# Scan phase of a two-layer image kernel: VectorE's half of the gate placed between two products, a z ring of six loaded two chunks ahead, a softplus ring of two

## The chip, the cores and the metric

The kernel runs on one core of one Trainium2 chip. The metric is device time in microseconds (us), the median of three runs. One further execution was taken by the hardware profiler; its page and trace are the source of every other number here. Five engines work side by side on a core: PE (TensorE, the matrix unit; its weight loads are shown as PEld), DVE (VectorE), ACT (ScalarE), POOL (GpSimd) and SP (SyncE, which here only issues DMAs). They wait for each other by semaphores, and each carries out its own instructions in the order in which they stand.

## The reference, cut to what matters

Input x is 8 images of 128 x 128 positions with 128 channels. Layer 0 is a linear attention block with a layer norm; layer 1 is a 2D selective scan (256 inner channels, one state per channel), and it is layer 1's last part that the change concerns:

```
xz = x @ Win;  xb, z = split(xz)                      # 256 channels each
xb = silu(depthwise_conv3x3(xb) + conv_b)
xs = [xb, reversed xb, turned xb, reversed turned xb] # 4 directions, L = 16384 positions
delta = softplus(dt_weight @ (Wxproj_dt @ xs) + dt_bias);  dA = exp(delta * A)
h[t] = dA[t] * h[t-1] + delta[t] * u[t] * B[t];   y[t] = h[t] * C[t] + u[t] * D
y = y0 + y1 + y2 + y3                                 # directions summed, each put back in place
yz = y * silu(z)                                      # the gate
out = layernorm(yz) @ Wout
```

The norm is over the 256 channels, so its mean and variance are sums over partitions, which PE takes with a matrix of 1/256.

## The kernel before, in words

Three stages follow each other. `layer0` computes layer 0 and silu(z), which goes to memory as `zs`. `layer1_front` does the convolution, the sums with D (`gs`), the products with B (`ubs`) and the small rows of the projection (`xps`). `layer1_scan` (from line 688) does the rest; only it is changed.

`layer1_scan` works in units. A unit is one chunk of 1024 positions (CH) of one scan: 8 output images x 4 directions ("places" 0 to 3) x 16 chunks (NCH) make 512 units. The sum y of one image, 256 channels x 16384 positions, stays in SBUF (`y`). Place 0 writes y, places 1 to 3 add to it. While place 0 of the next image runs over y, chunk by chunk, the finished image leaves just ahead of it: each of the 16 leaving steps takes one chunk of 1024 positions, as two pieces of 512 (hf 0 and 1), through gate, norm, projection and store.

The order of the work is written out by hand in `step(n)`; the block under `in_order` keeps every engine's instructions exactly in the order in which the program issues them. A step of unit n does the following. The line numbers are those of the profile.

- `emit(n - 1, hf)` on DVE: the products of the scan's result with C, which PE has spread over the partitions in PSUM (`pc`). In place 0 both halves go straight to y (L915, DVE). In the others half 0 goes to PSUM (L927 or L931) and `gather` adds it to y (L939); half 1 is made in `ubt` (L920), and POOL adds it (`add`, L946).
- `load_rows(n + 2)` (L851, L852) and `load` (ubt of unit n + 3, L858) on SP's queue. In place 0 ("first") `load` stands near the top of the step, in the others at its end.
- `decay` on ACT (exp, L877), `weigh` on POOL (ubt times softplus, L880), both halves of the channels.
- `scan(n, 0)` and `scan(n, 1)` on DVE (L887, L889).
- `delta(n + 1)` on PE (L869), `soften(n + 1)` on ACT (softplus, L873). Softplus and exp need different tables, so each step has two table loads on ACT.
- `spread` on PE (L903), C for the products of the next step.

For the image that leaves, with `now` the chunk of this step, `last` that of the step before and `soon` that of the next:

- `fetch` (L962, SP): both z pieces of a chunk, 512 KB each. The table `fetched` says in which step. Ring of five pieces.
- `gate` (L966): z := y * z, a piece of 2 x 512 on 128 partitions. Half 0 on POOL, half 1 on DVE, both at the end of the step before the chunk's own.
- `square` (L969, ACT) of both halves, written over y; `moments` (L979, PE); `keep` (L985, ACT) copies them; `to_tokens` (L991, PE); `square_mean` (L995, ACT, called mv); `variance` (L999, DVE), the last DVE work of a step but for the gate; `deviation` (L1003 and L1004, a power, POOL).
- `project` (L1011, PE): 32 small matmuls into a PSUM buffer of the ring of three (`px`).
- `store` in the next step (L1017, DVE, eight instructions in two buffers r; L1021, SP).
- `add_d` (L842, a DMA that POOL issues): adds the D sums `gs` to y in memory order, a chunk of 1 MB at a time, from 13 steps before the image leaves to 10 steps into the leaving.

`project` and `delta` share the ring `px`; `moments`, `to_tokens` and half 1 of `spread` share one PSUM bank (tag `pt`). After the last unit 17 more steps only let the last image leave.

The table of fetches before, with n the first leaving step of an image and j the chunk:

```
fetched[n + j - 2 if j > 1 else n + j - 4] = e
```

Of the kernel before, what the change touches and what calls it, by code (L numbers as in the profile page):

```python
# [8 lines left out]
F32 = mybir.dt.float32  # L9
# [7 lines left out]
P = 128  # L17
# [4 lines left out]
NC2 = 2  # L22
R = 8
K = 4
GW = 4
GN = GW * H
# [3 lines left out]
CH = 1024  # L30
CW = CH // H
NCH = L // CH
# [7 lines left out]
def split3(nc, parts, x):  # L40

    for j in range(3):
        nc.vector.tensor_copy(parts[j], x)
        if j < 2:
            nc.vector.tensor_tensor(x, x, parts[j], ALU.subtract)
# [640 lines left out]
def layer1_scan(ctx: ExitStack, tc, ubs, xps, zs, gs, dtw, dtb, a_log, gamma, beta, w_out, out):  # L686
# [15 lines left out]
    nc = tc.nc  # L702
    const = ctx.enter_context(tc.tile_pool(name="l2c", bufs=1))
    big = ctx.enter_context(tc.tile_pool(name="l2b", bufs=1))
    wp = ctx.enter_context(tc.tile_pool(name="l2w", bufs=3))
# [14 lines left out]
    D2 = 2 * P  # L720
    wparts = dram.tile([3, R, K, D2], BF16, name="wparts")
    bparts = dram.tile([3, K, D2], BF16, name="bparts")
    for dst, src, rows in ((wparts, dtw.rearrange("k r d -> r k d"), R), (bparts, dtb.rearrange("o (k d) -> o k d", d=D2), 1)):
        x = wp.tile([rows, K, D2], F32, name="w32", tag="sp", bufs=3)
        nc.sync.dma_start(x, src)
        q = wp.tile([rows, 3, K, D2], BF16, name="w16", tag="ub", bufs=4)
        split3(nc, [q[:, j] for j in range(3)], x)
        for j in range(3):
            if rows == 1:
                nc.sync.dma_start(dst[j : j + 1], q[:, j])  # L730
            else:
                nc.sync.dma_start(dst[j], q[:, j])
# [8 lines left out]
    for i in range(3):  # L741
        t = const.tile([P, CH], BF16, name=f"rows{i}")
# [3 lines left out]
    for i in range(2):  # L746
        t = const.tile([P, D2], BF16, name=f"dtw{i}")
# [23 lines left out]
            nc.vector.memset(sel[at : at + 1, hf, j : j + 1], 1.0)  # L771
    pb = pe.tile([P, P], F32, name="pbw", tag="pt")
    for c in range(NC2):
        bt = wp.tile([P, P], F32, name="bt", tag="z", bufs=5)
        nc.vector.tensor_copy(bt, gb[:, 1, c : c + 1].to_broadcast([P, P]))
        nc.tensor.matmul(pb, bt, wg[:, c, :], start=(c == 0), stop=(c == NC2 - 1))
    bw = const.tile([P, P], F32, name="bw")
# [59 lines left out]
    ubt, sp, da, st = {}, {}, {}, {}  # L837
# [6 lines left out]
    def load_rows(n):  # L844
        sl, i = units[n]
        m = sl.at(i)
        rw = rws[n % 3]
        md = NCH - 1 - m if sl.dt_turned_back else m
        src = xps[sl.dt_image, sl.dt_order].rearrange("j r l -> (j r) l")
        for j in range(3):  # L850
            nc.sync.dma_start(rw[3 * NR * j : 3 * NR * j + 3 * NR, :], src[:, md * CH : md * CH + CH])  # L851
        nc.sync.dma_start(rw[96:99, :], xps[sl.b, sl.order, :, R + 1, m * CH : m * CH + CH])  # L852

    def load(n):
        sl, i = units[n]
        m = sl.at(i)
        ubt[n] = wp.tile([P, NC2, CH], F32, name="ubt", tag="ub", bufs=4)
        nc.sync.dma_start(ubt[n], ubs[sl.b, sl.order].rearrange("c p l -> p c l")[:, :, m * CH : m * CH + CH])  # L858
# [10 lines left out]
            nc.tensor.matmul(p[:, hf * 512 : hf * 512 + 512], sl.dw[:, c * P : c * P + P], src, start=True, stop=True)  # L869

    def soften(n, c):
        sp[n, c] = t = wp.tile([P, CH], F32, name="sp", tag="sp", bufs=3)
        nc.scalar.activation(t, da[n, c], AF.Softplus)  # L873

    def decay(n, c):
        sl, i = units[n]
        nc.scalar.activation(da[n, c], sp[n, c], AF.Exp, scale=sa[:, sl.s, c : c + 1])  # L877

    def weigh(n, c):
        nc.gpsimd.tensor_tensor(ubt[n][:, c, :], ubt[n][:, c, :], sp.pop((n, c)), ALU.mult)  # L880
# [24 lines left out]
    def emit(n, hf):  # L905

        sl, i = units[n]
        h = ubt[n][:, :, hf * 512 : hf * 512 + 512]  # L910
        c = cps.pop((n, hf)).to_broadcast([P, NC2, GN])
        if sl.place == 0:
            v = sl.y_at(i, hf)
            split = "p c (a b) -> p c a b"
            nc.vector.tensor_tensor(v, h.rearrange(split, b=H), c.rearrange(split, b=H), ALU.mult)  # L915
            if hf == 1:
                ubt.pop(n)
            return
        if hf == 1:
            nc.vector.tensor_tensor(h, h, c, ALU.mult)  # L920
            return
        p = da.pop((n, 1))
        if sl.y_turned:
            ts[n] = p.rearrange("p (c b a) -> p c b a", c=NC2, a=GW)
            t = p.rearrange("p (c b a) -> p c a b", c=NC2, a=GW)
            split = "p c (a b) -> p c a b"
            nc.vector.tensor_tensor(t, h.rearrange(split, b=H), c.rearrange(split, b=H), ALU.mult)  # L927
        else:
            t = p.rearrange("p (c q) -> p c q", c=NC2)
            ts[n] = t.rearrange("p c (a b) -> p c a b", b=H)  # L930
            nc.vector.tensor_tensor(t, h, c, ALU.mult)  # L931

    def gather(n):

        sl, i = units[n]
        v = sl.y_at(i, 0)
        if sl.y_turned:
            v = v.rearrange("p c a b -> p c b a")
        nc.vector.tensor_tensor(v, v, ts.pop(n), ALU.add)  # L939
# [9 lines left out]
    zt, rst, pts, mv = {}, {}, {}, {}  # L949

    def piece(m, hf):
        return y[:, :, (2 * m + hf) * GN : (2 * m + hf + 1) * GN]

    def mirrored(o, m, hf):
        p = 2 * m + hf
        return 2 * NCH - 1 - p if o % 2 == 1 else p

    def fetch(o, m):
        for hf in range(2):
            zt[m, hf] = z = wp.tile([P, NC2, GN], F32, name="z", bufs=5)  # L960
            p = mirrored(o, m, hf)
            nc.sync.dma_start(z, zs[o].rearrange("c p l -> p c l")[:, :, p * GN : p * GN + GN])  # L962

    def gate(o, m, hf, eng):
        z, ym = zt[m, hf], piece(m, hf)
        eng.tensor_tensor(z, ym[:, :, ::-1] if o % 2 == 1 else ym, z, ALU.mult)  # L966

    def square(m, hf):
        nc.scalar.activation(piece(m, hf), zt[m, hf], AF.Square)  # L969
# [31 lines left out]
    def deviation(m):  # L1001
        rstd = rst[m]
        nc.gpsimd.tensor_scalar(rstd, rstd, 0.0, EPS1, ALU.max, ALU.add)  # L1003
        nc.gpsimd.tensor_tensor(rstd, rstd, half, ALU.pow)  # L1004
# [20 lines left out]
    leaving, summed, fetched = {}, {}, {}  # L1025
    for o in range(B):
        n = (o + 1) * K * NCH
        for j in range(NCH):
            e = o, NCH - 1 - j if o % 2 == 1 else j
            leaving[n + j] = e  # L1030
            fetched[n + j - 2 if j > 1 else n + j - 4] = e
            summed[n - NCH + 3 + (3 * j + 1) // 2] = e
    N = len(units)

    def step(n):
        live = 0 <= n < N
        then = n + 1 < N
        before = 1 <= n <= N
        now, last, soon = (leaving.get(n + i) for i in (0, -1, 1))
        first = before and units[n - 1][0].place == 0  # L1040
        if before:
            emit(n - 1, 0)
            if not first:
                gather(n - 1)
            emit(n - 1, 1)
        if n + 2 < N:
            load_rows(n + 2)
        if first and n + 3 < N:
            load(n + 3)
        if live:  # L1050
            for c in range(NC2):
                decay(n, c)
            weigh(n, 0)
        if last:
            deviation(last[1])
        if live:
            weigh(n, 1)
        if now:
            for hf in range(2):
                square(now[1], hf)  # L1060
            moments(now[1])
        if live:
            scan(n, 0)
            da.pop((n, 0))
        if last:
            for hf in range(2):
                store(*last, hf)
        if then:
            for c in range(NC2):
                delta(n + 1, c)  # L1070
        if now:
            keep(now[1])
        if then:
            for c in range(NC2):
                soften(n + 1, c)
        if now:
            to_tokens(now[1])
            square_mean(now[1])
        if live:
            scan(n, 1)  # L1080
            state(n)
        if now:
            variance(now[1])
        if live:
            spread(n, 0, "pc")
            spread(n, 1, "pt")
        if soon:
            gate(*soon, 0, nc.gpsimd)
            gate(*soon, 1, nc.vector)
        if now:  # L1090
            p = da.pop((n, 1)) if live else px.tile([P, CH], F32, name="px")
            for hf in range(2):
                project(now[1], hf, p[:, hf * 512 : hf * 512 + 512])
        elif live and units[n][0].place == 0:
            da.pop((n, 1))
        if before and not first:
            add(n - 1)
        if n + 3 < N and not first:
            load(n + 3)
        if live and units[n][1] == 1 and n - 1 + NCH < N:  # L1100
            units[n - 1 + NCH][0].weights()
        if n in summed:
            add_d(*summed[n])
        if n in fetched:
            fetch(*fetched[n])

    with in_order(tc):
        units[0][0].weights()
# [74 lines left out]
```

## Time and profile before

| what | value |
|---|---|
| median of 3 runs (lowest, highest) | 9721.64 us (9711.85, 9731.27) |
| profiled execution, its own time | 9691.45 us |
| its span, first to last instruction | 9689.7 us |
| DVE busy | 8237.5 us, 85% of the span |
| POOL busy | 7180.5 us, 74% |
| ACT busy | 7126.3 us, 74% |
| PE busy | 6369.1 us, 66% |
| DMA | 1851.21 MB, mean 191 GB/s |
| L966 on DVE: 128 instructions, mean (shortest, longest) | 2.263 us (1.221, 4.630) |
| L966 on POOL: 128 instructions, mean | 2.375 us |
| POOL's L966 waited for z | 100.6 us in 36 waits |
| DVE's L966 waited for z | 28.9 us in 21 waits |
| L999 on DVE waited for ACT's mv | 79.1 us in 49 waits |
| L1017 on DVE waited for the store of r | 25.4 us in 9 waits |

How to read it. Busy time is the time in which an engine has an instruction under way; an instruction that has started and then stands for a shared resource counts as busy. A line of the timeline gives start and duration in us, engine, line of the code, operation, out<-in, shapes and count, and in brackets how long the engine was idle before it and what ended that. The letter q after an engine's name means its sequencer: SPq L962 is the issue of z's load. A stretch's line has its two ends, its length, and then the busy times named with it. A waits line has who waited for whom: the sum in us, how often, and the longest.

### The profile page before, as it was taken

How to read it: one execution, taken by the hardware profiler on the slowest of the kernel's cores; microseconds unless marked ns; L12 is line 12 of the kernel's file. 1: busy time of each engine (PE TensorE's matmuls, PEld its weight loads, DVE VectorE, ACT ScalarE, POOL GpSimd, SP SyncE). 2: the span in 40 equal slices, each digit the busy share in tenths (PEclk: the TensorE clock that was granted, in tenths of full speed). 3: DMA queues.
4: the chain of work that ended last, by engine and by line, in shares of the span. 5: the costliest groups of instructions: out<-in, count | busy, mean ns of one | idle time of the engine just before them, and what ended most of it. 6: DMA issues, size and time to landing. Idle time of an engine off the chain costs nothing. (4 is left out here: it accounts for less than half of the span.)

```text
span 9689.7 us, 89952 instructions
## 1 busy us (share of the span) xinstructions
PE 6369.1 (66%) x24352; PEld 3134.8 (32%) x24352; DVE 8237.5 (85%) x8676; ACT 7126.3 (74%) x8226; POOL 7180.5 (74%) x4352
## 2 busy tenths in 40 slices
PE   8999999998877779777633634536355363543636
PEld 5555555554332223222200402304022040321403
DVE  6557775565988889888899999999999999999996
ACT  5556565555887778877788787787878878787784
POOL 3445554445575569776679899898989989899897
PEclk9999999999998889888855856658566585665857
DMA  2332233323576679887755948668486684957858
GB/s 90 133 131 86 86 133 131 132 99 117 195 253 225 235 267 247 262 262 266 271 161 170 267 149 232 202 177 255 152 239 194 189 246 152 257 179 193 238 155 214
DMA packets 1034807, 1851.21 MB, mean 191 GB/s; under 512 B 274852, under 2 KB 500772, under 8 KB 1026112
## 3 DMA queue, kind: packets, MB, share of 16 engines
q1 hardware_dynamic: 999488, 1711.23, 54.2%
q0 software_dynamic: 34816, 134.23, 7.1%
q8 instruction: 199, 3.26, 0.1%
q14 instruction: 304, 2.49, 0.1%
HBM read 1153.03 MB, written 692.12 MB: 190 GB/s over the span
## 5 line engine op out<-in xcount | busy, mean ns | idle before, releaser
L880 POOL TENSOR_TENSOR ubt<-ubt,sp 128x1024 f32<-128x1024 f32 x1024 | 2446.6, 2437 | 188.8 <-ACT sp L873 163.1
L869 PE MATMUL px<-rows,dtw 128*128 128x512 bf16 x2048 | 947.9, 564 | 2251.3 <-DVE y L939 1014.6
L504 POOL TENSOR_TENSOR tap<-tap 128x1024 f32<-128x1024 f32 x512 | 1206.8, 2368 | 634.3 <-ACT tap L502 516.7
L512 DVE SCALAR_TENSOR_TENSOR acc<-xb,cw,acc 128x1024 f32<-128x1024 f32 x1024 | 1320.4, 1289 | 52.7 <-DVE acc L512 0.5
L873 ACT ACTIVATE sp<-px 128x1024 f32<-128x1024 f32 x1024 | 1035.2, 1024 | 408.0 <-PE px L869 325.9
L946 POOL TENSOR_TENSOR y<-y,ubt 128x512 f32<-128x512 f32 x768 | 1156.2, 1542 | 149.8 <-DVE ubt L920 148.2
L494 PE MATMUL acc<-xi,wt 128*128 128x512 f32 x2048 | 952.7, 608 | 383.5 <-ACT ures L519 383.1
L869 PEld LDWEIGHTS <-dtw 128*128 128x128 bf16 x2048 | 166.8, 110 | 3070.2 <-issue 960.7
L887 DVE TENSOR_TENSOR_SCAN ubt<-px,state,ubt 128x1024 f32<-128x1024 f32 x480 | 1105.5, 2334 | 4.9 <-issue 3.6
L889 DVE TENSOR_TENSOR_SCAN ubt<-px,state,ubt 128x1024 f32<-128x1024 f32 x480 | 1104.3, 2334 | 6.1 <-issue 3.6
L877 ACT ACTIVATE px<-sp,sa 128x1024 f32<-128x1024 f32 x1024 | 1103.3, 1109 | 6.1
L502 ACT ACTIVATE tap<-xb,cw 128x1024 f32<-128x1024 f32 x768 | 834.3, 1139 | 68.6 <-POOL tap L504 67.5
L873 ACT ACT_TABLE_LOAD x512 | 656.9, 1283 | 226.0 <-PE px L869 207.9
L274 POOL TENSOR_TENSOR q<-q,qs 128x512 f32<-128x512 f32 x256 | 271.1, 1059 | 669.0 <-DVE qs L273 667.8
L494 PEld LDWEIGHTS acc<-xi,wt 128*128 128x128 f32 x2048 | 384.0, 192 | 928.4 <-ACT ures L519 485.6
L877 ACT ACT_TABLE_LOAD x512 | 656.9, 1283 | 9.4
L1011 PEld LDWEIGHTS px<-wg,z 128*128 128x128 f32 x4096 | 588.8, 229 | 165.5 <-issue 159.5
L903 PE MATMUL pc<-rows,csel 128*128 128x512 bf16 x1024 | 516.4, 585 | 129.3 <-DVE rstd L999 126.6
L1011 PE MATMUL px<-wg,z 128*128 128x128 f32 x4096 | 587.4, 312 | 0.0
L467 PE MATMUL pxb<-xi,wi 128*128 128x512 f32 x1024 | 496.2, 607 | 4.5 <-ACT xb L476 4.3
L939 DVE TENSOR_TENSOR y<-y,px 128x1024 f32<-128x1024 f32 x384 | 468.6, 1220 | 14.2
L290 ACT ACTIVATE sq<-o 128x512 f32<-128x512 f32 x256 | 161.2, 630 | 421.6 <-DVE o L288 420.4
(158 smaller groups left out, 15323.6 us busy)
## 6 DMA issues: line engine op xcount, KB each, us to landing
ubt<-ubs SPq DMA_DIRECT2D x512, 1024.0 KB
zs<-z SPq DMA_DIRECT2D x512, 256.0 KB
ubs<-ures SPq DMA_DIRECT2D x256, 512.0 KB
ubs<-turned SPq DMA_DIRECT2D x256, 512.0 KB
y<-gs POOLq DMA_DIRECT2D x128, 1024.0 KB, 11.9
z<-zs SPq DMA_DIRECT2D x256, 512.0 KB
rows<-xps SPq DMA_DIRECT2D x1536, 60.0 KB
xi<-x SPq DMA_DIRECT2D x120, 576.0 KB
```

The lines of the kernel that those rows point to most:

```text
L494: nc.tensor.matmul(acc[:, s, :], wt[:, j, c, :], x, start=(j == 0), stop=(j == len(ON_PE) - 1))
L502: nc.scalar.activation(t, at(n, c, *d), AF.Copy, scale=cw[:, c, tap(*d) : tap(*d) + 1])
L504: nc.gpsimd.tensor_tensor(sums[n, c], sums[n, c], t, ALU.add)
L512: nc.vector.scalar_tensor_tensor(acc, at(n, c, *d), cw[:, c, tap(*d) : tap(*d) + 1], acc, ALU.mult, ALU.add)
L869: nc.tensor.matmul(p[:, hf * 512 : hf * 512 + 512], sl.dw[:, c * P : c * P + P], src, start=True, stop=True)
L873: nc.scalar.activation(t, da[n, c], AF.Softplus)
L877: nc.scalar.activation(da[n, c], sp[n, c], AF.Exp, scale=sa[:, sl.s, c : c + 1])
L880: nc.gpsimd.tensor_tensor(ubt[n][:, c, :], ubt[n][:, c, :], sp.pop((n, c)), ALU.mult)
L887: nc.vector.tensor_tensor_scan(e[:, ::-1], x[:, ::-1], e[:, ::-1], start, ALU.mult, ALU.add)
L889: nc.vector.tensor_tensor_scan(e, x, e, start, ALU.mult, ALU.add)
L946: nc.gpsimd.tensor_tensor(v[:, c], v[:, c], h[:, c], ALU.add)
L1011: nc.tensor.matmul(po[:, w, :], z[:, c, w * H : w * H + H], wg[:, c, :], start=(c == 0), stop=(c == NC2 - 1))
```

## The change

Four edits, all in `layer1_scan`:

1. DVE's half gate of a chunk moves from the end of the step before (`gate(*soon, 1)`, after the scans and the variance) into the chunk's own step, after `emit(n - 1, 0)` (and `gather`, where there is one) and ahead of `emit(n - 1, 1)`. POOL's half stays where it was. The DVE instructions are the same in number and kind.
2. The fetch of z moves from the end of a step to a place behind `load_rows` and `load`, so ahead of the store of r in SP's queue. Chunks 3 to 15 are still fetched two steps ahead of their own; chunks 0, 1 and 2 are fetched 20 steps before their own step, which is in the last four steps of place 2. Before, chunks 0 and 1 were fetched four steps ahead, and chunk 2 two.
3. The z ring has six pieces (three chunks) instead of five.
4. The softplus ring has two buffers instead of three; 4 KB per partition go from one ring to the other.

```diff
-        sp[n, c] = t = wp.tile([P, CH], F32, name="sp", tag="sp", bufs=3)
+        sp[n, c] = t = wp.tile([P, CH], F32, name="sp", tag="sp", bufs=2)
...
-            zt[m, hf] = z = wp.tile([P, NC2, GN], F32, name="z", bufs=5)
+            zt[m, hf] = z = wp.tile([P, NC2, GN], F32, name="z", bufs=6)
...
-            fetched[n + j - 2 if j > 1 else n + j - 4] = e
+            fetched[n + j - (2 if j > 2 else NCH + 4)] = e
...
             emit(n - 1, 0)
             if not first:
                 gather(n - 1)
+        if now:
+            gate(*now, 1, nc.vector)
+        if before:
             emit(n - 1, 1)
         if n + 2 < N:
             load_rows(n + 2)
         if first and n + 3 < N:
             load(n + 3)
+        if n in fetched:
+            fetch(*fetched[n])
...
         if soon:
             gate(*soon, 0, nc.gpsimd)
-            gate(*soon, 1, nc.vector)
...
         if n in summed:
             add_d(*summed[n])
-        if n in fetched:
-            fetch(*fetched[n])
```

The two other edited lines give the setup's tiles of the same rings (w32 and bt) the new ring sizes.

More of the change, by code (lines that the diff above doesn't have):

```diff
@@ L723, in layer1_scan @@
     for dst, src, rows in ((wparts, dtw.rearrange("k r d -> r k d"), R), (bparts, dtb.rearrange("o (k d) -> o k d", d=D2), 1)):
-        x = wp.tile([rows, K, D2], F32, name="w32", tag="sp", bufs=3)
+        x = wp.tile([rows, K, D2], F32, name="w32", tag="sp", bufs=2)
         nc.sync.dma_start(x, src)
@@ L773, in layer1_scan @@
     for c in range(NC2):
-        bt = wp.tile([P, P], F32, name="bt", tag="z", bufs=5)
+        bt = wp.tile([P, P], F32, name="bt", tag="z", bufs=6)
         nc.vector.tensor_copy(bt, gb[:, 1, c : c + 1].to_broadcast([P, P]))
```

## The prediction

> **What bounds the kernel now.** I read the busy table and the 40 slices first, then stretches, then the timeline of single steps, then the waits. The scan phase runs from 4870 us to 9538 us: 512 steps, and a tail of 17. The stretches are one image position of 64 steps: place 0 (16 steps in which the finished image also leaves), places 1, 2, 3, the next place 0, and the tail. Columns: length, busy time of PE, weight loads, VectorE, ScalarE, GpSimd, PE clock, DMA share, GB/s.
>
> ```profile
> 5382.90:5574.40 191.50, 146.99 (x969) 106.28 (x966) 180.61 (x230) 148.28 (x161) 162.97 (x88) 0.90 0.91 269
> 5574.40:5708.90 134.50, 49.49 (x123) 12.11 (x121) 132.36 (x104) 109.31 (x97) 125.35 (x64) 0.53 0.49 152
> 5708.90:5840.30 131.40, 46.78 (x97) 9.00 (x96) 130.17 (x97) 108.33 (x96) 125.33 (x64) 0.50 0.49 152
> 5840.30:5976.70 136.40, 46.07 (x97) 9.45 (x98) 131.72 (x98) 107.05 (x96) 125.98 (x74) 0.50 0.82 218
> ...
> 9538.20:9689.70 151.50, 122.15 (x896) 85.59 (x896) 63.32 (x163) 43.90 (x64) 90.04 (x59) 0.93 0.78 205
> ```
>
> Places 1 and 2 are packed: 8.2 us a step, VectorE 99% busy. What the change touches lies in place 0 (12.0 us a step), the end of place 3, and the tail. But VectorE's 94% in place 0 is not all work. A clean gate, with what GpSimd does beside it, and a bad one:
>
> ```profile
> 5559.72 2.35 POOL L880 TENSOR_TENSOR ubt<-ubt,sp 128x1024 f32<-128x1024 f32 x1 [1.38 <-ACT sp L873]
> ...
> 5560.84 2.31 DVE L966 TENSOR_TENSOR z<-y,z 128x1024 f32<-128x1024 f32 x1
> ...
> 5562.03 1.23 POOL L1003 TENSOR_SCALAR rstd<-rstd 128x8 f32<-128x8 f32 x1
> ```
>
> ```profile
> 6676.73 2.36 POOL L966 TENSOR_TENSOR z<-y,z 128x1024 f32<-128x1024 f32 x1 [2.08 <-DMA z<-zs]
> ...
> 6679.02 1.27 POOL L842 DMA_DIRECT2D y<-gs  x1
> ...
> 6679.41 2.78 SPq L962 DMA_DIRECT2D z<-zs  x2
> 6679.46 4.33 DVE L966 TENSOR_TENSOR z<-y,z 128x1024 f32<-128x1024 f32 x1
> ...
> 6679.89 2.81 POOL L880 TENSOR_TENSOR ubt<-ubt,sp 128x1024 f32<-128x1024 f32 x1
> ...
> 6682.23 1.67 POOL L1003 TENSOR_SCALAR rstd<-rstd 128x8 f32<-128x8 f32 x1
> ```
>
> The gate's own work is 1.1 to 1.2 us (shortest of all 128: 1.221). In the clean case it stands 1.2 us until GpSimd's product (L880) ends at 5562.07, then runs while L1003, which lasts 0.24 us alone at 6659.14, is stretched to 1.23. In the bad case z landed late, GpSimd's half gate and its DMA issue slid, and L880 took the port first: 4.33 us. At the end of place 3 (PE, then VectorE), and the two other waits that matter:
>
> ```profile
> 6553.14 1.87 PE L869 MATMUL px<-rows,dtw 128*128 128x512 bf16 x4 [7.97 <-DMA rows<-xps]
> ...
> 6555.47 1.23 DVE L931 TENSOR_TENSOR px<-ubt,pc 128x1024 f32<-128x1024 f32 x1 [1.60 <-PE pc L903]
> ```
>
> ```profile
> 6651.58 1.12 DVE L1017 SCALAR_TENSOR_TENSOR r<-px,rstd,bw 128x128 f32<-128x128 f32 x4 [1.77 <-DMA out<-r]
> ```
>
> ```profile
> SPq L962 <- PE px L1011: 54.0, 13, 6.2
> ```
>
> The last is SP's own wait in one place 0 (6571 to 6765): 54 us at the head of the z loads, with rows, ubt and everything else behind.
>
> **What the Trainium skill says.** "SBUF — State Buffer", Who interferes with whom: a VectorE instruction with two SBUF inputs contends with a GpSimd instruction that reads SBUF, and the second fully blocks. The two gates above agree (2.31 and 4.33 against 1.22); the products with pc in PSUM show no such spread (1.21 us). "DMA: Bandwidth & Descriptors", Queues, rings and completion order: each DMA engine consumes a ring in order; so a small load issued behind z waits for it. The 7.97 us above, with z issued 5.6 us before, fits. "Perfetto Trace Analysis", GPSIMD Engine Instruction: take GpSimd times from start to start; two L880 in a row give 2.35 us that way (4.70 for the pair), as their spans say.
>
> **The change, part by part.** *The loop that stays.* I measure from the end of the variance (L999), V, to the next. In a clean step ScalarE runs: table load and decays to V+3.25, squares to V+5.2, waits for the moments until V+7.15, copy, table load, softplus, mean square at V+11.1, then V'. None of this moves. PE adds a second leg: projection to V+4.0 at full clock, V+5.6 or V+6.8 at a lower one, then 1.9 us of moments. So a step can't go below about max(7.15, projection end + 1.92) + 4.2. Over the 105 intervals of seven place 0s the timeline gives 11.99 us on average, this formula, fed with each one's projection end, 11.66; 27 intervals lie over 0.3 us above it.
>
> *Gate between the products.* VectorE's work without the gate is 9.0 us start to start (products 2.27, scans 4.56, r 2.05, small ones 0.15). The gate now starts at V+1.17. When ScalarE sets the pace, L880 ends at V+1.25 (softplus half 0 ends 1.2 us before V, plus 2.44), so I take 0.1 us of lock wait and 1.1 us of work: VectorE needs 10.2 us instead of 11.25, and is no longer the limit. The gate ends at V+2.4, before square half 1 is due at V+4.25: nothing is late behind it. The second product, queued behind it, ends at V+3.5 instead of V+4.65, so the bank of the moments and the ubt slot come free sooner. Bounds: no wait, 10.1 us; a gate that meets the power (L1004, 1.66 us) instead waits up to 1.7, VectorE then needs 11.8.
>
> *Loads two chunks ahead.* SP's order was rows, ubt, out, z, z waiting for this step's projection; now rows, ubt, z, out, the slot freed a step before. z is issued near V+5 of step n for GpSimd's gate near V'+6.6, 13 us instead of about 5. The late-z gates go: 35.2 us over 105 intervals, all that the formula leaves. The DMA engines are at 0.91 over place 0 and above 1.0 for steps at a time, so I take **28 us**; bounds 0 and 83 (every step at 11.2).
>
> *z of three chunks loaded before place 3.* It leaves the last four steps of place 3, where gs and z together made rows late, and goes into place 2 (share 0.49, about 4.0 us of 8.2 a step; another 1 MB at about 270 GB/s is 3.9, for three steps: it fits, cost 0; bound 1 us a step). From the scan of the last but one step to V of the leaving step took 17.1 us (6549.1 to 6566.2); two clean steps less the products are 12.9, and GpSimd's gate (2.35) and DMA issue (1.2), which stay, leave it about 0.6 late: 13.5. 8 × 3.6 = **28 us** (bounds 10 and 36).
>
> *First leaving step.* V to V was 14.3 us (6566.20 to 6580.48), since softplus was late after the rows; with rows in time squares end near V+5.8 (two products, gate, square), so 12.2. 7 × 2.1 = **15 us** (bounds a loss of 5, since GpSimd is in L880 then and the gate may stand 2.4 us; a gain of 20).
>
> *Tail.* 16 steps in 151.5 us. PE alone needs 7.35 (9612.07 to 9619.42); GpSimd's gate stood up to 9.8 us for its z (9604.46), issued at the end of the step before. With z ahead PE needs 16 × 7.35 = 118, the DMA engines 0.78 × 151.5 = 118. Both can't be packed: 131, **20 us** (bounds 0 and 30).
>
> *Softplus ring of two.* Softplus half 1 now waits for GpSimd's product of the step before: in place 2 that ends at 5708.74, the softplus starts at 5712.39. 3.6 us of cover: 0. If GpSimd fell 4 us behind, ScalarE would wait the rest, and decays, squares and the scan behind it (bound 1 us at 8 boundaries).
>
> Sum: 28 + 28 + 15 + 20 = 91 us, so the profiled execution (9691.45, span 9689.7 and 1.8 around) would be 9600. It lies 30 us under the median; from 9721.64 the same 91 give **9631**.
>
> **Rivals.** (1) *PE and DMA follow at once*: every drain step near 11.3, boundaries and tail at their bounds, 73 + 36 + 20 + 30 = 159: 9563. For it: ScalarE's loop. Against: DMA share, the projections at lower clock. (2) *The transfers are the limit*: place 0 stays near 12.0 because DMA is already full, and only boundaries and half the tail gain: 28 + 10 = 38: 9684. For it: shares of 1.0 and more over several steps; against: steps of 11.2 at a share of 1.02. (3) *Slower: out lands behind z.* r has two buffers, so a step can't be shorter than the landing time of an out plus 1.2 us. out now stands behind 1 MB of ubt and 1 MB of z. If an out takes over 10.8 us, the step passes 12.0; at 13 us it is 14.2, in the 11 steps with gs: 2.2 × 11 × 7 = 169, less 28 + 15 + 20: 106 us slower, 9828. For it: the 1.77 us above, and loads of 10 to 15 us in the chain. Against: ubt, z and gs were as many before, and only 25 us went to this wait in all.
>
> **Chances.** Forecast 0.62 (9590 to 9675), rival 1 0.13, rival 2 0.16, rival 3 0.09. About 0.2% (19 us) is what a measurement tells from no change. Of rival 2's 0.16, 0.09 lies beyond that and 0.07 within; of rival 3's 0.09, 0.01 within: faster 0.84, same 0.08, slower 0.08. The range reaches to rival 1 and past rival 2: 9568 to 9708.
>
> **What would show it.** Right: gates of VectorE near 1.2 to 1.4 us; no wait of either gate for z; SP's wait for the projection gone; L999 waiting for mv about 0.8 us in each step; rows no longer late at the ends of place 3, place 3 near 132 us; place 0 near 186; tail near 131. Wrong: gates still at 2.3 (the meeting with L880 or L1004); r waiting for out step after step; softplus waiting for GpSimd in places 1 and 2.

## The result, and the profile after

| what | before | after |
|---|---|---|
| median of 15 runs (lowest, highest) | 9709.78 us (9698.72, 9731.27) | 9696.08 us (9684.92, 9708.34) |
| ratio, 95% interval | | 0.9984 [0.9977, 0.9991] |
| span of the profiled execution | 9689.7 us | 9696.4 us |
| first scan to the end | 4819.8 us | 4814.7 us |
| tail, end of the last scan to the end | 151.5 us | 143.8 us |
| VectorE waited for z / GpSimd waited for z | 28.9 / 100.6 us | 0 / 1.9 us |
| L999 waited for mv | 79.1 us | 139.3 us |
| r (L1017) waited for the store of r | 25.4 us | 93.8 us |

The kernel became faster by 14 us; 91 were forecast. (The forecast of 9631 us was counted from a median of 3 runs; that of 15 lies 12 us lower.) The span of the profiled run says nothing on this: 12 us of it lie ahead of the first scan, in code that the change doesn't touch, and the profiled execution of before was 18 us faster than its median, that of after 2 us slower. So I compare from the first scan on, and trust the medians for the total. The same stretches as before, with the same columns: places 0 to 3 and the tail.

```profile
5396.40:5586.30 189.90, 150.11 (x963) 108.48 (x980) 163.11 (x232) 145.30 (x159) 159.21 (x86) 0.86 0.84 258
5586.30:5719.60 133.30, 47.40 (x111) 10.55 (x112) 132.13 (x103) 109.14 (x97) 125.31 (x64) 0.52 0.49 152
5719.60:5851.00 131.40, 46.13 (x95) 9.02 (x96) 130.16 (x96) 108.34 (x96) 125.33 (x64) 0.50 0.56 176
5851.00:5989.50 138.50, 45.07 (x93) 8.94 (x94) 137.26 (x97) 110.13 (x98) 129.62 (x75) 0.50 0.83 212
...
9552.50:9696.40 143.90, 115.37 (x896) 81.50 (x896) 60.23 (x164) 43.35 (x63) 91.73 (x58) 0.95 0.81 212
```

VectorE lost 17.5 us of busy time in place 0 (180.6 to 163.1), but place 0 lost 1.6 us only. Place 3 is longer, 138.5 in place of 136.4, and its added time is booked as VectorE work (137.3 in place of 131.7). Place 2 takes the early z (share 0.56 in place of 0.49) at no cost.

First what went as forecast, in the timeline of one step: the gate starts 0.2 us before the product L880 ends (6592.22 + 2.35 = 6594.57) and lasts 1.28 us. 120 of VectorE's 128 gates are now 1.21 to 1.30 us long.

```profile
6592.22 2.35 POOL L880 TENSOR_TENSOR ubt<-ubt,sp 128x1024 f32<-128x1024 f32 x1 [4.56 <-ACT sp L873]
...
6594.38 1.28 DVE L966 TENSOR_TENSOR z<-y,z 128x1024 f32<-128x1024 f32 x1
...
6594.55 1.22 POOL L1003 TENSOR_SCALAR rstd<-rstd 128x8 f32<-128x8 f32 x1
```

Now the first gate of the same image, one step earlier in the same timeline:

```profile
6575.05 5.53 POOL L880 TENSOR_TENSOR ubt<-ubt,sp 128x1024 f32<-128x1024 f32 x2
...
6576.85 7.11 DVE L966 TENSOR_TENSOR z<-y,z 128x1024 f32<-128x1024 f32 x1
...
6579.66 3.21 POOL L966 TENSOR_TENSOR z<-y,z 128x1024 f32<-128x1024 f32 x1
6583.88 1.21 DVE L920 TENSOR_TENSOR ubt<-ubt,pc 128x1024 f32<-128x1024 f32 x1
6584.00 1.06 ACT L969 ACTIVATE y<-z 128x1024 f32<-128x1024 f32 x1 [5.22 <-DVE z L966]
```

It needs 1.1 us of work and takes 7.11. It ends at 6583.96, which is 1.09 us after GpSimd's own half gate ends (6582.87): it stood through two products and that gate, and ScalarE waited 5.22 us for it. It is so in seven images (7.11 to 7.22 us); the eighth took 2.61. Before the change this gate took 1.40 to 1.43 us in all eight; the same one in the timeline of before:

```profile
6563.56 3.47 POOL L946 TENSOR_TENSOR y<-y,ubt 128x512 f32<-128x512 f32 x2
...
6564.49 1.41 DVE L966 TENSOR_TENSOR z<-y,z 128x1024 f32<-128x1024 f32 x1
```

The second surprise is the store. The timeline of the third leaving step, of SP's queue and VectorE:

```profile
6611.90 0.39 SPq L858 DMA_DIRECT2D ubt<-ubs  x1
...
6612.62 0.89 SPq L962 DMA_DIRECT2D z<-zs  x2
...
6613.48 1.22 POOL L842 DMA_DIRECT2D y<-gs  x1
6613.60 1.57 SPq L1021 DMA_DIRECT2D out<-r  x2
...
6627.05 2.16 DVE L1017 SCALAR_TENSOR_TENSOR r<-px,rstd,bw 128x128 f32<-128x128 f32 x8 [5.38 <-DMA out<-r]
```

The store is issued at 6613.60 behind 1 MB of ubt and 1 MB of z, and the next r can be written only at 6627.05, 13.4 us later. In the packet records of the trace, the store's 1024 packets of 512 B (512 KB, both halves) move between 6623.9 and 6627.0, after ubt (6612.9 to 6617.8) and beside the last of z (6616.5 to 6625.5). Most of that time went by beside the 1 MB of gs: from 6619 to 6623 its packets took 0.80 to 0.82 of the 16 engines' time and those of z 0.23 to 0.25, and the store stood behind z. What the wait would be without gs no run tells, since none moves gs. The variance-to-variance interval of this step is 16.1 us on the mean of seven images, 13.3 before. The waits of the whole run:

```profile
DVE rstd L999 <- ACT mv L995: 139.3, 113, 5.7
...
DVE r L1017 <- DMA out<-r: 93.8, 33, 9.8
...
POOL z L966 <- DMA z<-zs: 1.9, 2, 1.5
```

Where the time went, in us, from the starts of the scans. "Start" is the eleven steps from ten before an image leaves to its first leaving step, of seven images; "leaving" the other 15 steps of place 0, of seven images; "end" the last ten steps with the tail. "Forecast" sorts the prediction's terms the same way (28 × 7/8 + 15; 28; 20 + 28/8; the ring 0).

| | before | after | difference | forecast |
|---|---|---|---|---|
| start | 716.6 | 706.5 | -10.1 | -39.5 |
| leaving | 1243.7 | 1257.7 | +14.0 | -28 |
| end | 232.7 | 222.3 | -10.4 | -23.5 |
| all other steps | 2626.7 | 2628.1 | +1.4 | 0 |

One profiled run scatters in these sums: b2 below, which measures like the kernel before, has 719.7, 1255.5, 232.0, 2630.4. Against b2, "leaving" of the changed kernel is only 2.2 us longer. So the +14 is weak by itself; that the -28 is missing is not.

### The profile page after: what moved, and what is told of

It is laid out like the page before. It is cut to its first block, busy times and chain, and to the rows that moved or that the text cites. A ratio compares the mean times of both kernels' runs of the same rounds, so it can differ in the third digit from the quotient of the medians.

```text
span 9696.4 us, 89952 instructions
## 1 busy us (share of the span) xinstructions
PE 6347.2 (65%) x24190; PEld 3133.0 (32%) x24352; DVE 8158.9 (84%) x8676; ACT 7127.9 (74%) x8226; POOL 7169.8 (74%) x4352
## 5 line engine op out<-in xcount | busy, mean ns | idle before, releaser
L880 POOL TENSOR_TENSOR ubt<-ubt,sp 128x1024 f32<-128x1024 f32 x1024 | 2433.4, 2429 | 266.7 <-ACT sp L873 248.4
L869 PE MATMUL px<-rows,dtw 128*128 128x512 bf16 x1893 | 912.6, 575 | 2191.0 <-DVE y L939 1029.3
L873 ACT ACTIVATE sp<-px 128x1024 f32<-128x1024 f32 x1024 | 1037.0, 1024 | 441.2 <-PE px L869 354.1
L946 POOL TENSOR_TENSOR y<-y,ubt 128x512 f32<-128x512 f32 x768 | 1147.2, 1529 | 169.3 <-DVE ubt L920 164.6
L939 DVE TENSOR_TENSOR y<-y,px 128x1024 f32<-128x1024 f32 x384 | 468.6, 1220 | 14.2
```

The lines of the kernel that those rows point to most:

```text
L946: nc.gpsimd.tensor_tensor(v[:, c], v[:, c], h[:, c], ALU.add)
```

## The experiments

Three theories. **P, the port:** the first gate of an image is caught behind GpSimd's unbroken train of work, and pays for most of what the earlier rows bring. **Q, the queue:** the store of r, now issued behind z, lands too late for the next r. **R, the transfers:** the DMA engines are full in place 0, in whatever order things are issued. All ratios are to the kernel before on the same chip.

**a1, first gate back at the end of the step before** (only chunk 0's):

```diff
-        if now:
+        if now and last:
             gate(*now, 1, nc.vector)
...
             gate(*soon, 0, nc.gpsimd)
+            if not now:
+                gate(*soon, 1, nc.vector)
```

> The changed kernel with one thing put back: chunk 0's half gate on VectorE stands at the end of the step before, as in the kernel before; chunks 1 to 15 stay between the products. Theory P (the shared port): in the changed kernel that first gate stands about 5.9 us behind GpSimd's three products and gates in a row, in 7 images; put back, it takes about 1.4 us, the step from the scan before it to the next goes from 15.3 back to near 9.6 us, and the time falls by 30 to 40 us against the changed kernel, to a ratio of about 0.995 with the kernel before. Theory Q (out behind z): the first gate is cheap to remove but the step after it is held by other waits; at most 10 us fall. Theory R (the transfers are full anyway): what the gate gives back is lost again in the next steps to waits for out; 0 to 10 us.

9694.14 us, ratio 0.9982 [0.9975, 0.9989]: nothing gained, a miss. The timeline shows why:

```profile
5969.79 2.90 POOL L946 TENSOR_TENSOR y<-y,ubt 128x512 f32<-128x512 f32 x2
...
5972.12 9.79 DVE L966 TENSOR_TENSOR z<-y,z 128x1024 f32<-128x1024 f32 x1
...
5972.22 1.63 POOL L842 DMA_DIRECT2D y<-gs  x1
...
5972.99 5.53 POOL L880 TENSOR_TENSOR ubt<-ubt,sp 128x1024 f32<-128x1024 f32 x2
...
5977.60 3.22 POOL L966 TENSOR_TENSOR z<-y,z 128x1024 f32<-128x1024 f32 x1
```

The gate starts 2.7 us earlier against the first L880 (0.87 us ahead of it, where after has it 1.80 behind) and still ends 1.09 us after GpSimd's own half gate (5981.91 against 5980.82): 9.7 to 9.8 us in five images. In two others it slipped in at once (1.57 and 1.71 us). The old place had been good only with the old timing: in the kernel before, rows were late, so the gate met GpSimd in the sums L946 and got in between the two of them, in all eight images. The stand behind several GpSimd instructions, as P has it, is seen again; the place that I took for free was not.

**a2, the z loads behind the store in SP's queue**, still two chunks ahead:

```diff
-        if n in fetched:
-            fetch(*fetched[n])
...
         if n in summed:
             add_d(*summed[n])
+        if n in fetched:
+            fetch(*fetched[n])
```

> The changed kernel with the loads of z put back behind the store of r in SP's queue, still two steps ahead and in the ring of six. Theory Q: r's waits for out (65.6 us in place 0 and 28 in the tail, by the profile of the changed kernel) go to under 25 us; the third leaving step falls from 16.1 to about 12 us; 30 to 45 us less than the changed kernel, ratio to before 0.994 to 0.996. Theory R: the wait only moves, to rows or z that now stand behind more; no gain over 10 us. Theory P alone: no change, since VectorE's order is the same.

9666.69 us, ratio 0.9955 [0.9943, 0.9968]: 28 us better than the changed kernel by the ratios, and in the range named for Q. The timeline of the corresponding step:

```profile
6590.15 0.38 SPq L858 DMA_DIRECT2D ubt<-ubs  x1
...
6590.86 2.80 SPq L1021 DMA_DIRECT2D out<-r  x2
...
6594.56 0.90 SPq L962 DMA_DIRECT2D z<-zs  x2
...
6603.74 2.13 DVE L1017 SCALAR_TENSOR_TENSOR r<-px,rstd,bw 128x128 f32<-128x128 f32 x8
```

r no longer waits here; the store's packets move from 6595.4 to 6599.0, so they have landed 8.1 us after the issue, with most of z behind them and gs not begun (6600.0). Over the run r's waits for the store fall from 93.8 to 27.1 us, 25.4 of them in the tail. The third interval is 11.8 us, "leaving" 1214.4, that is 29.3 under before. Q is shown, and R falls: the same bytes move.

**a3, both edits.**

> Both of the above: chunk 0's gate at the end of the step before, and z behind out in SP's queue. Theories P and Q together: the gains add, 60 to 80 us less than the changed kernel, ratio to before about 0.990 to 0.992; place 0 near 186 us, tail near 138. Theory R: less than 20 us.

9666.68 us, ratio 0.9955 [0.994, 0.997]: no better than a2, a miss against 0.990 to 0.992, and after a1 it had to be one (first gates 9.7 to 9.8 us).

**a4, the kernel before with VectorE's gate between the products and nothing else** (edit 1 of the change).

> The kernel before with only VectorE's half gate moved between the two products (all chunks); z ring of five, its loads at the end of a step, softplus ring of three. Theory P: chunks 1 to 15 win (gates 1.3 us instead of 2.3, no late gates on VectorE), about 20 us over 105 steps, chunk 0 loses about 5.9 us x 7 = 41: a net loss of 10 to 30 us, ratio 1.001 to 1.003. If the gate's place alone were a gain (the intent of the change), the ratio would be 0.997 or less.

9700.58 us, ratio 0.9996 [0.9987, 1.0005]: no difference, where 0.1 to 0.3% of loss was expected. One first gate took 6.94 us, six took 2.19 and the last 3.58. The timeline of the long one, then of a short one:

```profile
5973.15 1.16 POOL L842 DMA_DIRECT2D y<-gs  x1
5974.21 4.77 POOL L880 TENSOR_TENSOR ubt<-ubt,sp 128x1024 f32<-128x1024 f32 x2
...
5975.44 6.94 DVE L966 TENSOR_TENSOR z<-y,z 128x1024 f32<-128x1024 f32 x1
...
6567.34 1.18 POOL L842 DMA_DIRECT2D y<-gs  x1
...
6568.68 5.65 POOL L880 TENSOR_TENSOR ubt<-ubt,sp 128x1024 f32<-128x1024 f32 x2 [0.16 <-ACT sp L873]
...
6569.90 2.19 DVE L966 TENSOR_TENSOR z<-y,z 128x1024 f32<-128x1024 f32 x1
```

Both gates met the same queue, two products and the half gate. In all six short cases GpSimd had first stood idle for 0.16 to 0.53 us, since the rows and with them softplus were late, and the gate got in between the two products. In the long case GpSimd came from its DMA issue without a pause, and the gate stood to the end. So what is queued on GpSimd doesn't decide by itself how long the gate stands.

**b1, the reverse: the change without its gate edit.**

> The changed kernel with VectorE's half gate back at the end of every step, the loads two chunks ahead and both rings as changed. If the new place of the gate is worth nothing by itself (what the prediction said, cover only), the time is the changed kernel's: ratio to the kernel before 0.997 to 1.000, gates 2.2 to 2.4 us in the steady steps, the third store of an image still about 13 us under way, r still waiting some 60 us for out in place 0. If the shorter gates are what holds off a loss from the earlier loads, ratio 1.002 to 1.006.

9720.65 us, ratio 1.0010 [1.0002, 1.0019], between the two ranges named. The earlier loads without the gate's move lose 10 us. The changed kernel differs from b1 by the gate's place alone, and is 0.26% faster. About a third of that lies in the first gates: at the old place six of the seven stand 9.7 to 9.8 us, and the step before the first leaving one takes 16.5 us in place of 15.3. The rest is spread over the leaving steps and the tail. There L999 waits less for mv (84.3 us in b1, 139.3 in the changed kernel), so VectorE has less slack in which to hide a wait for the store; that this is why the move pays here is argued, not shown.

**b2, the softplus ring of two alone** (`bufs=3` to `bufs=2` on the tag sp).

> The kernel before with a softplus ring of two and nothing else. The prediction set this part at 0. If the third buffer was never used, ratio 0.999 to 1.001. If ScalarE ran two products ahead of GpSimd anywhere in the scan, the steps of places 1 and 2 grow by 0.1 us or more, 512 steps give 50 us: ratio 1.005.

9710.59 us, ratio 0.9999 [0.9991, 1.0007]: 0, as forecast.

**d1, GpSimd's half gate behind its last sum**, so that its train has two members:

```diff
-        if soon:
-            gate(*soon, 0, nc.gpsimd)
...
         if before and not first:
             add(n - 1)
+        if soon:
+            gate(*soon, 0, nc.gpsimd)
```

> The changed kernel with GpSimd's own half gate issued behind its last sum of the step before, so that the train of L880, L880, L966 ends after the second L880 (the sum L946 that follows waits for VectorE). Theory P, VectorE's first gate of an image stands until GpSimd's unbroken train ends: chunk 0's gate 4.2 to 4.8 us in place of 7.1, interval of that step about 12.5 in place of 15.3, ratio to the kernel before 0.995 to 0.998 (gain of 7 times 2.5 us on the changed kernel, less what GpSimd's later half gate costs the leaving steps). Rival, the first gate waits for its data or for something else than the port: it stays at 7 us. A loss of up to 0.4% is possible if GpSimd's half gate now ends after ScalarE needs z; the length of the first gates decides, not the total.

9674.17 us, ratio 0.9961 [0.9946, 0.9975]; all seven gates are 4.82 to 4.92 us long, just over the 4.2 to 4.8 named. The timeline:

```profile
6566.20 5.16 POOL L880 TENSOR_TENSOR ubt<-ubt,sp 128x1024 f32<-128x1024 f32 x2
...
6567.63 4.83 DVE L966 TENSOR_TENSOR z<-y,z 128x1024 f32<-128x1024 f32 x1
...
6573.66 2.50 POOL L946 TENSOR_TENSOR y<-y,ubt 128x512 f32<-128x512 f32 x2 [2.30 <-DVE ubt L920]
```

L880 ends at 6571.36, the gate at 6572.46, 1.10 us later. Neither its data nor its own place was changed, only what GpSimd has queued behind the products, so it is GpSimd's queue that it waits for. The step became 13.0 us long in place of 15.3.

**c1, a2 with the first gate six steps earlier**, where GpSimd's two products are followed by a sum that waits for VectorE:

```diff
-        if now:
+        if now and last:
             gate(*now, 1, nc.vector)
+        if n + 6 in leaving and n + 5 not in leaving:
+            gate(*leaving[n + 6], 1, nc.vector)
```

> The kernel with the store ahead of z in SP's queue (a2), and chunk 0's VectorE gate six steps earlier, where GpSimd runs only the two L880 of the step and then waits for VectorE. Theories P and Q together: first gates about 2 to 4.5 us in place of 7.2, taken out of the first leaving step, place 3 about 133 to 135 us, the intervals around the start of an image 3 to 5 us shorter in 7 images: 25 to 35 us under a2, ratio 0.991 to 0.993. If the first gate's stand was not on the path that sets the end, the ratio stays at a2's 0.9955.

9634.24 us, ratio 0.9920 [0.9908, 0.9933], as forecast. The gate again ends 1.1 us after the second L880 (6513.58 against 6512.48), but it starts late enough to stand 1.5 us only:

```profile
6507.30 5.18 POOL L880 TENSOR_TENSOR ubt<-ubt,sp 128x1024 f32<-128x1024 f32 x2
...
6511.03 2.55 DVE L966 TENSOR_TENSOR z<-y,z 128x1024 f32<-128x1024 f32 x1
```

Its places 0 and 3 and its tail, in the columns of before:

```profile
5391.90:5577.40 185.50, 148.09 (x957) 106.60 (x972) 166.78 (x230) 146.37 (x160) 164.53 (x88) 0.88 0.92 273
...
5843.40:5977.90 134.50, 45.42 (x95) 9.12 (x98) 132.78 (x98) 108.92 (x97) 125.10 (x74) 0.50 0.80 206
9494.20:9640.20 146.00, 117.07 (x896) 81.78 (x896) 62.89 (x162) 42.88 (x63) 88.20 (x58) 0.96 0.80 209
```

**d2, the edits of a2 and d1 together.**

> The two cures of a2 and d1 together: the store of the finished chunk ahead of the z load in SP's queue, and GpSimd's half gate behind its last sum. If the port (P) and the queue (Q) are two separate losses, they add: the third interval at 11.6 to 12 us as in a2, the first gate at 4.8 us as in d1, and 15 us (from d1's steps around an image, 7 times 2.1) to 22 us (from d1's total) under a2: ratio to the kernel before 0.993 to 0.994. If they are one loss seen in two places, the ratio stays at a2's 0.9955.

9645.23 us, ratio 0.9932 [0.9919, 0.9946]. Under the changed kernel a2 gave 0.29%, d1 0.23%; together 0.52%. P and Q are two separate losses, and they add within the intervals. (The third interval is 12.4 us, a little over the 11.6 to 12 named.)

**c2, c1 with z first again in the tail.**

> c1, but with z loaded ahead of everything else in the tail's 17 steps, as the changed kernel has it, and behind the store in the other steps. In the tail nothing else is loaded but z, so the loads should not cost the store much, and VectorE's waits for z (10.5 us in c1's tail) should go: tail 136 to 144 us in place of 146, ratio 0.991 to 0.992. If the store's wait takes back what z gives (the changed kernel's tail: 143.8 us with 28 us of r waiting for out), nothing is left: ratio 0.992.

9625.15 us, ratio 0.9912 [0.9897, 0.9928]: the lowest median of all, but its interval overlaps c1's. The tail is 144.8 us in place of 146.0, just over the 136 to 144 named; VectorE's waits for z are gone, and r waits 35.3 us for the store in their place. So the tail trades one wait for the other.

**f1, the store issued from ScalarE's queue** behind the mean square, z first as in the changed kernel, first gate as in c1:

```diff
-        nc.sync.dma_start(dst[:, s, :], r)
+        return lambda: nc.scalar.dma_start(dst[:, s, :], r)
...
             square_mean(now[1])
+        if last:
+            for s in ship:
+                s()
```

> c1's early first gate, z loaded ahead as in the changed kernel, but the store of the finished chunk issued from ScalarE's queue, behind the mean square, instead of SP's. It asks what Q's delay is made of. If the store was late because it stood behind ubt and z in one queue (order), it lands soon although z is issued first: VectorE's waits for out 5 us or less over place 0, place 0 about 185 us an image, and in the tail, too, neither z nor the store is late: tail 130 to 140, ratio to the kernel before 0.990 to 0.992. If it was late because the transfer engines are full whichever queue it comes from, the third interval stays near 16 us and r waits some 60 us, as in the changed kernel: ratio 0.994 to 0.995. A cost on ScalarE, which paces these steps, by the issue of two stores: 0.1 us each, 16 steps, 8 images: up to 26 us, ratio 0.994 without any wait for out.

9749.38 us, ratio 1.0037 [1.0024, 1.0051]: a clear miss. A queue of its own doesn't bring the store forward. The timeline of the third leaving step:

```profile
6610.72 0.39 SPq L858 DMA_DIRECT2D ubt<-ubs  x1
...
6611.22 1.98 SPq L962 DMA_DIRECT2D z<-zs  x2
6611.43 0.38 ACTq L1021 DMA_DIRECT2D out<-r  x1
...
6611.90 1.13 ACTq L1021 DMA_DIRECT2D out<-r  x1
...
6622.76 1.13 DVE L1017 SCALAR_TENSOR_TENSOR r<-px,rstd,bw 128x128 f32<-128x128 f32 x4 [4.68 <-DMA out<-r]
...
6625.34 1.13 DVE L1017 SCALAR_TENSOR_TENSOR r<-px,rstd,bw 128x128 f32<-128x128 f32 x4 [1.46 <-DMA out<-r]
```

Issued at 6611.43, the store's packets begin at 6615.8 and need until 6624.7, mixed with those of ubt, gs and z; in each us from 6616 to 6625 they get 0.05 to 0.32 of the engines' time. From issue to the next write of its buffer a half takes 11.3 and 13.4 us, against 13.4 and 13.6 in the changed kernel. The third interval is 16.8 us, and r waits 171.4 us in the run. This is what the Trainium skill says in "DMA: Bandwidth & Descriptors", Issuing engines are not separate DMA queues: transfers of all issuing engines run on the same 16 DMA engines and interleave. So Q isn't a matter of the queue's order alone: what else is under way counts, whoever issued it. But the ratio isn't the price of the queue alone. Behind the mean square a store is issued 2.6 us after its r is ready on the mean of place 0, against 0.2 us in the changed kernel, and an issue on ScalarE's queue lasts 0.38 us in the median, where 0.1 was assumed; that part wasn't taken apart. That the first packet moves only 4.4 us after the issue is not peculiar to ScalarE's queue: ubt, issued on SP's at 6610.72, begins at 6614.6, while gs has 0.7 to 1.04 of the engines' time. What holds them back wasn't tested.

**b3, the port:** a3 with every leaving step's next gate behind the first scan.

> One look at the port alone: a3 with VectorE's half gate of the next chunk issued in the leaving steps right behind the first scan, just as GpSimd runs the product L880 and goes on without a pause to its own half gate L966. If VectorE has to wait for the end of GpSimd's unbroken train, these gates take 4 to 5.5 us; if the two engines take turns instruction by instruction, 2.3 to 3.1 us; if they share, 1.2 to 2 us. Its time: slower than a3 by 0.1 to 0.5% where the gate no longer stands in VectorE's idle time.

9877.86 us, one run. Its time tells nothing on the port, since these gates waited 173.0 us for z in place 0, now that they are issued earlier than their load lands. The gates themselves tell something:

```profile
6628.25 2.35 POOL L880 TENSOR_TENSOR ubt<-ubt,sp 128x1024 f32<-128x1024 f32 x1
...
6629.64 2.04 DVE L966 TENSOR_TENSOR z<-y,z 128x1024 f32<-128x1024 f32 x1
6630.57 3.34 POOL L966 TENSOR_TENSOR z<-y,z 128x1024 f32<-128x1024 f32 x1
```

This gate waits for the end of L880 (6630.60), and then runs 1.08 us, while GpSimd's half gate, next in its train, is 1.0 us longer than its usual 2.36. So here, as in a4, VectorE came in between two GpSimd instructions that follow each other without a pause, and "the train keeps the port" is no rule.

## Why the prediction was wrong, point by point

The changed kernel (after) and the kernel with both faults taken out (c1) against the forecast, as differences to before in us:

| | forecast | after | c1 |
|---|---|---|---|
| start | -39.5 | -10.1 | -35.4 |
| leaving | -28 | +14.0 | -27.4 |
| end | -23.5 | -10.4 | -5.6 |
| all other steps | 0 | +1.4 | +7.5 |
| sum | -91 | -5.1 | -60.9 |

The columns are single profiled executions against another, and before's was 18 us under its median; by the ratio c1 is 78 us faster (0.80% of 9709). The measured 9696 us lies in the stated range, and rival 2 (9684, the transfers are the limit) came nearest to it, but by luck: a2 moves the same bytes and is 28 us faster.

Two steps of the prediction failed: the first gate was priced at no wait, and out of the way it gives 34 us (c1 against a2, by the ratios); the store behind z stood in a rival but at nothing in the sum, and out of the way it gives 28 us (a2 against the changed kernel). The tail was over-priced by some 12 us.

- *The loop that stays; the gate between the products.* Right. Over the 105 intervals of c1 the formula, fed with the ends of the projections, gives 11.65 us and the trace shows 11.65. Gates are 1.2 to 1.3 us. That the move alone brings nothing was right too (a4).
- *Loads two chunks ahead, 28 us.* The mechanism was right and the size about right: a2 has -29.3, c1 -27.4 (measured from b2 in place of before, 12 us more). The gain failed to come in the changed kernel because rival 3 came in beside it. "If an out takes over 10.8 us, the step passes 12.0; at 13 us it is 14.2, in the 11 steps with gs" had the right landing time (13.4 us), but not the number of steps: on the mean only the third interval of an image is much longer than the formula (16.1 us against 11.5), and two others by 0.7 and 0.9. In the third step ubt, z, gs and the store are all issued within 1.7 us (6611.90 to 6613.60). I had treated the forecast and this rival as either-or; they are two terms of one sum.
- *First leaving step, 15 us, and z of three chunks before place 3.* The second of these came in full: from the scan of the last step but one to the first product of the first leaving step, 17.5 us on the mean of seven images became 12.9, where 13.5 was forecast. The first failed. From that product to V it had 14.7 us and was to have 12.2; it has 18.9. "Bounds a loss of 5, since GpSimd is in L880 then and the gate may stand 2.4 us" priced the wait at one GpSimd instruction, because a gate in place 0 meets one. At the end of place 3 it meets two products and the half gate, with a DMA issue just ahead: 7.1 us, 6.0 of them standing. With the rows in time (the last step but one takes 8.21 us, 10.8 before), the next step grew from 11.2 to 15.3. With the gate out of the way the gain of both terms is there: c1 has 35 of the 39.5 us, and 12.8 us from the product to V. I had looked at the first gate only as the old timing showed it, and this very change moved the timing.
- *Tail, 20 us.* The 131 was a guess between 118, which PE or the transfers need alone, and 151.5. Too large; the changed kernel gained 7.7 us in it, and no kernel went below 143.8. With z first the store is late (28.2 us in the changed kernel's tail, 35.3 in c2's); with the store first z is late. Why PE and the transfers can't be packed closer is not settled: no experiment here tells whether a third buffer of r would end it.
- *Softplus ring, 0.* Right (b2).
- *Signs named beforehand.* Gates short: seen. z waits gone: seen. SP's wait for the projection: smaller, 131 us in the run in place of 399, not gone. L999 waiting for mv: seen, 1.1 us a step in place of 0.8. r waiting for the store: seen, mostly in the third leaving step. Place 3 near 132: missed at 138.5, 134.5 in c1. Place 0 near 186: 189.9, and 185.5 in c1.

## What to carry to other kernels

When a change takes a wait away, draw the step again with the new times before pricing what is left in it: an instruction that met a free resource by luck of the old timing may now meet a busy one. Bound the wait for a shared port by all that its other user has queued without a pause, not by the one instruction seen beside it (a4 shows that the wait can be shorter), and put the operation next to a place where the other engine has to wait. When a load is moved earlier, look for what is issued right behind it with a small ring: let the small store go first, as a2 does; moving it to another queue with a later issue (f1) made it worse.

## What the runs showed of the hardware

- The Trainium skill, "SBUF — State Buffer", Who interferes with whom, calls the pair of ports that VectorE and GpSimd share an exclusive lock, and says that a VectorE instruction with two SBUF inputs contends with a GpSimd instruction that reads SBUF. The runs agree for one instruction (2.31 us in before, 2.04 us in b3), and show a longer stand: a VectorE product with two SBUF inputs was held through two (4.8 us) and three (7.1 us) GpSimd instructions, and through the end of a sum, a DMA issue and three more (9.8 us).
- When does it get in between two of them? I counted all ends of GpSimd instructions that a gate met after standing for at least 0.1 us, with a further GpSimd instruction directly behind (without the small L1003 and L1004), in all fourteen profiled kernels. 161 times the gate began there, and the next GpSimd record started at most 0.12 us before the one before it ended. 174 times it stood on, and the records overlapped by 0.16 to 0.95 us. The two never mix, and they are not tied to the pair of instructions: two L880 in a row are found on both sides. In these traces the overlap thus shows which GpSimd instructions run as one for VectorE.
- What differs is what GpSimd did before. In all 174 cases it had issued a DMA (L842, `add_d`) since it last stood idle; in 158 of the 161 it had not. The instruction behind L842 overlaps it by 0.36 us more than L842 overlaps the one before (median), and the overlap then mostly stays until GpSimd has to wait. Whether the DMA issue is the cause, no run tells: none moves it. Moving `add_d` off this place is the experiment that is missing.
- A store of 512 KB in packets of 512 B, which takes 3.2 us when its turn comes, landed 13.4 us after its issue behind 2 MB of loads just issued and beside 1 MB of gs, and 8.1 us behind 1 MB of ubt and the rest of an older z (a2).
